# A vision tower on one core: tokenizer differences taken from PSUM, first units as rows come, and unread products in four waits of TensorE

## The chip, the cores and the metric

The kernel runs on one NeuronCore of a Trainium2 chip. The metric is device time in microseconds of one execution, and lower is better. The engines are TensorE (PE, with PEld for its weight loads), VectorE (DVE), ScalarE (ACT), GpSimd (POOL) and SyncE (SP, which only issues transfers here). Each engine works through its own list of instructions in order and waits on semaphores for the others. L12 is line 12 of the kernel.

## The reference, cut to what matters

A batch of 128 images of 128 x 128 goes through a tokenizer (two strided convolutions, each followed by a batch normalization) and two layers. All is float32.

```python
x = _bn(_conv(X, w1, 8), g1, b1, m1, v1)          # 8x8 patches, 64 channels
x = _bn(_conv(x, w2, 2), g2, b2, m2, v2)          # 4x4, stride 2, 256 channels
h = tokens(x)                                     # (128, 64, 256)
h = h + _L0_attn_ref(_layernorm(h), ...)          # sum_d relu(q - k) w_d, softmax, values
h = h + _L0_ffn_ref(_layernorm(h), ...)           # attention by 4 soft experts
h = h + _L1_attn_ref(_layernorm(h), ...)          # linear attention over the batch
h = h + _L1_ffn_ref(_layernorm(h), ...)           # 8 experts, one for each token, capacity 1280
```

In the last step each token goes to the expert with the largest gate; `pos`, a running count of the tokens of each expert, gives its place, and places past the capacity are dropped.

## The kernel before, in words

The stages follow one another: `tokenizer` (0 to 181 us of the span), `relu_attention` (to about 1116), `expert_attention` (to about 1945), `linear_attention` (to about 2275), `route` (to 2324) and `experts`.

**Tokenizer.** Sixteen rows of patches come in one after another (`load`, L82, three buffers). `conv1(r)` (L130) makes two float32 products of 512 columns with the weights `w1bd`, which hold the 64 x 64 matrix twice on the diagonal: an even half and an odd half, each in a PSUM tile `pa`. The even half is scaled and offset by ScalarE into `ev` (L135), shifted by one position on the upper 64 partitions, where a memset has left a zero at the border. The odd half is scaled and offset by VectorE into `h[:, 0:4]` (L132). `differences(r)` then forms even minus odd and odd minus the next even on VectorE (L141, L142). These sums and differences serve a scheme that does the 4-tap second convolution with three products in place of four in each direction. `between` (L151, L154) forms differences of two rows, on GpSimd except for one that VectorE and one that ScalarE takes.

A `Unit(m, ab)` is a quarter of the output channels for two output rows. It has three sets of products, `products(0)`, `(1)` and `(2)` (L177, tile `pc`[...]), each with one ScalarE reading (L189) and one or two VectorE readings (L204, L200), and two `results` (L210), where the scale of the second normalization comes in. Products 0 need the row differences `between(m, 0, ...)`, products 1 the rows themselves and `w02`, products 2 `between(m, 2, ...)`.

The order on each engine is written out by hand (`tc.manual_schedule()`): rows 0 to 4 go through `conv1` and `differences` first, with the row differences of the first units, and only then come the 16 units, each with one more row in front of it as long as there are rows.

**End of attention.** The last block of queries goes through `less_max`, `exponents`, `sums`, `weights` (VectorE, ScalarE, VectorE, GpSimd L535) and then `transpose` on TensorE (L544), `transposed` (ScalarE L552). After it come the products with the values (`po`, L441), their copies (L452), transposes (`pto`, L459) and the additions to `h` (L469). The PSUM pool `psq` (tag `pq`, three buffers) is the one for keys, values and the transposes at a block's beginning.

**Routing.** `route` computes probabilities and places on VectorE. Two small products (`pp`, L1684, L1685) add up the counts across partitions; `past` (L1735) and `bexp` (L1739) give each block of 256 tokens its expert. Then a table of the tokens' numbers by place is made by 64 products `pi` (L1733) of two one-hot matrices: `lh` (L1723) and `hv` (L1726) come from VectorE in groups of eight, two buffers of each, ScalarE multiplies `hv` by the token numbers (L1731), and TensorE sums. The indices `rin` and `rout` (L1742 to L1746) are read from `pi`.

**Experts.** Each block of 256 tokens is gathered by GpSimd (`gather`, L1810), normalized (`moments` L1820, `normal` L1828), transposed (`pt` L1841, copy `xt` L1844), and goes through two layers (`ph` L1853, `po` L1869). Weights come by SP (L1797, L1798), three blocks deep.

Of the kernel before, what the change touches and what calls it, by code (L numbers as in the profile page):

```python
# [26 lines left out]
BLK = 256  # L27
# [4 lines left out]
class Ctx:  # L32
# [3 lines left out]
    def __init__(self, tc, const):  # L36
# [6 lines left out]
        self.zero = const.tile([P, 8], F32, name="zero")  # L43
        nc.vector.memset(self.zero, 0.0)

    def tables(self, const):


        self.rin = const.tile([P, NTILE], I32, name="rin")
        self.rout = const.tile([P, NTILE], I32, name="rout")  # L50
        self.bexp = const.tile([P, NBLK + 1], I32, name="bexp")


def bcast(ap, axis, n):

    v = ap.unsqueeze(axis)
    shape = list(v.shape)
    shape[axis] = n
    return v.to_broadcast(shape)


def tokenizer(c, x, w1, bn1, w2, bn2):
# [6 lines left out]
    with (  # L69
# [2 lines left out]
        tc.tile_pool(name="th", bufs=8) as hp,  # L72
        tc.tile_pool(name="tv", bufs=6) as vp,
        tc.tile_pool(name="tz", bufs=2) as zp,
        tc.tile_pool(name="tp1", bufs=2, space=PSUM) as ps1,
        tc.tile_pool(name="tp2", bufs=3, space=PSUM) as ps2,
    ):
        rows = {}
# [4 lines left out]


        w1bd = wp.tile([P, P], F32, name="w1bd")
        nc.vector.memset(w1bd, 0.0)
        bnv1 = wp.tile([P, 4], F32, name="bnv1")
        bnv2 = wp.tile([P, 4, 4], F32, name="bnv2")
        for k in range(2):
            nc.sync.dma_start(w1bd[k * 64 : (k + 1) * 64, k * 64 : (k + 1) * 64], w1)  # L90
            nc.sync.dma_start(bnv1[k * 64 : (k + 1) * 64, :], bn1)
        load(0, nc.scalar)
        for r in range(1, 3):
            load(r)
# [22 lines left out]
        for ev in evens:  # L117
            nc.gpsimd.memset(ev[0:64, 4], 0.0)
            nc.gpsimd.memset(ev[64:128, 0], 0.0)

        parts = {}

        def conv1(r):

            xt = rows.pop(r)
            parts[r] = h = hp.tile([P, 12, B], F32, tag="h", name="h")
            ev = evens[r % 3]
            for k in range(2):
                pa = ps1.tile([P, 4, B], F32, tag="pa", name="pa")
                nc.tensor.matmul(pa, w1bd, xt[:, 4 * k : 4 * k + 4], start=True, stop=True)  # L130
                if k:
                    nc.vector.tensor_scalar(h[:, 0:4], pa, s1, o1, ALU.mult, ALU.add)  # L132
                else:
                    for o, i in ((ev[0:64, 0:4], slice(0, 64)), (ev[64:128, 1:5], slice(64, P))):
                        nc.scalar.activation(o, pa[i], AF.Identity, bias=o1[i], scale=s1[i])  # L135
            if r + 3 < 16:
                load(r + 3)

        def differences(r):
            h, ev = parts[r], evens[r % 3]  # L140
# [21 lines left out]
        class Unit:  # L162
# [6 lines left out]
            def products(self, i):  # L169
                m, ab = self.m, self.ab  # L170
                pc = ps2.tile([P, 4, 4, N], F32, tag="pc", name="pc")
                for j, j0 in ((1, 0), (0, 4), (2, 8)):
                    for k in range(2):
                        u = w02[:, k, j] if i == 1 else w[:, k + i, j]
                        for par in range(2):
                            r = slice(par * 64, par * 64 + 64)
                            nc.tensor.matmul(  # L177
                                pc[r, j],
                                u[:, ab * 64 : ab * 64 + 64],
                                part(m, i, k)[:, j0 : j0 + 4, r],  # L180
                                start=(k == 0),
                                stop=(k == 1),
                            )
# [5 lines left out]
                nc.scalar.activation(  # L189
                    y,  # L190
                    pc[:, 1].rearrange("p o n -> p n o"),
                    AF.Identity,
                    bias=o2[:, a] if i == 1 else 0.0,
                    scale=s2[:, a] if i == 1 else 1.0,
                )
                o = self.z[:, i].rearrange("p n (o q) -> p n o q", q=2)
                x = pc[:, 0::2].rearrange("p q o n -> p n o q")
                if i == 1:
                    for q in range(2):
                        nc.vector.scalar_tensor_tensor(  # L200
                            o[:, :, :, q], x[:, :, :, q], s2[:, a], y, ALU.mult, ALU.add
                        )
                else:
                    nc.vector.tensor_add(o, x, bcast(y, 3, 2))  # L204

            def results(self, k):

                ab = self.ab
                f = ab // 2 * 128 + (2 * self.m + k) * 16 + ab % 2 * 8
                nc.vector.scalar_tensor_tensor(  # L210
                    h2[:, :, f : f + 8],
                    self.z[:, 2 * k],
                    (s2, n2)[k][:, ab : ab + 1],
                    self.z[:, 1],
                    ALU.mult,
                    ALU.add,
                )

        with tc.manual_schedule():
            for r in range(5):  # L220
                conv1(r)
                if r == 1:
                    nc.gpsimd.tensor_add(w[:, :, 1], w[:, :, 0], w[:, :, 2])
                differences(r)
                if r == 1:
                    nc.scalar.mul(w[:, :, 2], w[:, :, 2], -1.0)
                    nc.gpsimd.tensor_add(w02, w[:, 0:2], w[:, 2:4])
                    between(0, 0, 0)
                elif r == 2:
                    between(0, 0, 1)  # L230
            for k in range(2):
                between(0, 2, k)
# [27 lines left out]
def relu_attention(c, wqkv, wmlp, bmlp):  # L260
# [8 lines left out]
    with (  # L269
# [387 lines left out]
        with tc.manual_schedule():  # L657
# [978 lines left out]
def route(c, k, gfd):  # L1636
# [5 lines left out]
    with (  # L1642
# [56 lines left out]
        nc.vector.tensor_sub(first, end, nblk)  # L1699
        nc.vector.tensor_scalar_mul(first, first, float(BLK))  # L1700


        nc.vector.tensor_add(cs, cs, bcast(pp[:, 0], 1, T))
        nc.vector.scalar_tensor_tensor(oh, cs, float(CAP), oh, ALU.is_le, ALU.mult)
# [14 lines left out]
        for t0 in range(0, T, T // NQ):  # L1719
# [11 lines left out]
                nc.scalar.activation(hv[:, i], hv[:, i], AF.Copy, scale=k.token[:, t])  # L1731
            for i in range(T // NQ):
                nc.tensor.matmul(pi, lh[:, i], hv[:, i], start=(t0 + i == 0), stop=(t0 + i == T - 1))  # L1733
            if t0 == 0:
                nc.vector.tensor_tensor(past, bcast(k.blk, 2, E), bcast(end, 1, NBLK), ALU.is_ge)  # L1735
                nc.vector.tensor_reduce(be[:, 0:NBLK], past, AX.X, ALU.add)
                nc.vector.tensor_scalar_min(be[:, 0:NBLK], be[:, 0:NBLK], float(E - 1))
                nc.vector.tensor_copy(be[:, NBLK : NBLK + 1], end[:, E - 1 : E])
                nc.vector.tensor_copy(c.bexp, be)  # L1739
# [9 lines left out]
def experts(c, hx, gfd, out, w1, w2, b2, routing):  # L1749
# [9 lines left out]
    with ExitStack() as nest:  # L1759
# [138 lines left out]
        with tc.manual_schedule():  # L1898
            for n in range(2):
                blocks[n].load()  # L1900
            for n in range(2):
                blocks[n].gather((False,))
            blocks[0].moments()
            blocks[0].normal()
            blocks[0].transpose()
            for n in range(2):
                blocks[n].gather((True,))
            blocks[1].moments()
            blocks[2].gather()
            blocks[1].normal()  # L1910
# [42 lines left out]
def layout(**i):  # L1953
# [9 lines left out]
    o["w1"] = i["L0_tok_w1"].reshape(64, 64)  # L1963
    o["bn1"] = np.stack([i[f"L0_tok_{k}1"] for k in "gbmv"], axis=1)
# [5 lines left out]
    o["bn2"] = bn2.reshape(4, 8, 2, 8, 2).transpose(1, 3, 0, 2, 4).reshape(64, 4, 4)  # L1970
    q, k, v = (i[f"L0_attn_W{n}"].T for n in "qkv")

    v = v.reshape(D, 32, 8).transpose(0, 2, 1).reshape(D, D)
# [45 lines left out]
```

## Time and profile before

| | us |
|---|---|
| median of three runs | 2759.32 (2752.79 to 2761.09) |
| profiled execution | 2759.04 |
| its span | 2757.1 |
| mean granted clock of TensorE | 0.972 |
| busy: TensorE, VectorE, GpSimd, ScalarE | 2599.0, 2037.6, 1631.1, 1627.6 |

The profiled execution is one run; its time is 1.9 us more than its span, which reaches from the first instruction to the last. A line of the timeline has the start, the length, the engine, the source line, the operation, the output and inputs, the shapes, how many instructions are merged, and in brackets how long the engine was idle before it and what ended that idle time. A line of a table of stretches has the stretch, its length, the busy time of PE, PEld, DVE, ACT and POOL with the number of instructions, the granted clock (1.00 is full), the DMA share and GB/s. A float32 product leaves two records.

### The profile page before, as it was taken

The numbers are of one execution on the slowest core, as the hardware profiler recorded it, in microseconds if no ns is written. First come the engines' busy times: TensorE is split into PE (matmuls) and PEld (weight loads), VectorE is DVE, ScalarE is ACT, GpSimd is POOL, SyncE is SP. The second block draws the span as 40 slices with busy tenths as digits, with TensorE's granted clock in tenths as the row PEclk, the third lists the DMA queues.
The fourth block names the chain that finished last, engine by engine and source line by source line (L and its number), as shares of the span: only waits on it lengthen the run. The fifth ranks groups of instructions, "written<-read, shape, count | busy, mean of one in ns | idle before, by whom it ended". The sixth has DMA issues, their size and how long they took to land. (4 is left out here: it accounts for less than half of the span.)

```text
span 2757.1 us, 76948 instructions
## 1 busy us (share of the span) xinstructions
PE 2599.0 (94%) x33263; PEld 1741.0 (63%) x33263; DVE 2037.6 (74%) x3024; ACT 1627.6 (59%) x3415; POOL 1631.1 (59%) x1390
## 2 busy tenths in 40 slices
PE   7989999999999999799999999999699986999997
PEld 3553434434444443688888888888466565888886
DVE  6759999999998989577877777777367685344443
ACT  3228888888898888366666666566245543233332
POOL 3328888898888888656566565553233312454444
PEclk9999999999999999799999999999899995999999
DMA  3000000000000000000000000000424443555554
GB/s 108 32 12 2 2 1 2 2 2 2 1 2 1 2 2 1 12 11 18 11 11 18 11 15 14 10 19 11 115 62 112 102 120 114 180 197 189 188 196 134
DMA packets 138063, 140.80 MB, mean 51 GB/s; under 512 B 107923, under 2 KB 121509, under 8 KB 130032
## 3 DMA queue, kind: packets, MB, share of 16 engines
q1 hardware_dynamic: 126816, 117.91, 14.3%
q0 software_dynamic: 7648, 14.77, 1.7%
q8 instruction: 263, 4.31, 0.7%
q10 hardware_dynamic: 3248, 3.09, 0.4%
q14 instruction: 88, 0.72, 0.1%
HBM read 103.93 MB, written 32.54 MB: 49 GB/s over the span
## 5 line engine op out<-in xcount | busy, mean ns | idle before, releaser
L495 POOL TENSOR_TENSOR m<-q,k 128x1024 f32<-128x1024 f32 x384 | 719.0, 1903 | 30.5 <-PE sc L297 16.1
L487 DVE TENSOR_TENSOR m<-pc,k 128x2048 f32<-128x2048 f32 (+1 forms) x320 | 646.7, 2058 | 0.5 <-ACT q L431 0.5
L297 PE MATMUL sc<-m,wide 128*32 128x512 f32 x4096 | 529.5, 598 | 12.0 <-DVE m L487 7.2
L496 ACT ACTIVATE m<-m 128x1024 f32<-128x1024 f32 x384 | 402.3, 1049 | 6.0 <-POOL m L495 5.4
L297 PEld LDWEIGHTS sc<-m,wide 128*32 128x32 f32 x4096 | 126.4, 109 | 259.7 <-issue 145.6
L505 ACT ACTIVATE m<-k,q 128x64 f32<-128x64 f32 x1024 | 270.8, 339 | 0.8 <-DVE k L378 0.8
L946 DVE TENSOR_REDUCE mx<-sc 128x16 f32<-128x1024 f32 x128 | 156.1, 1220 | 153.9 <-PE sc L934 123.7
L961 POOL TENSOR_TENSOR e<-e,mx 128x1024 f32<-128x1024 f32 x128 | 243.5, 1902 | 10.1 <-POOL mx L960 0.2
L906 ACT COPY qk<-pqk 128x512 f32<-128x512 f32 x256 | 138.9, 604 | 131.7 <-PE pqk L902 131.7
L960 POOL TENSOR_TENSOR mx<-mx,gate 128x16 f32<-128x16 f32 x128 | 27.6, 216 | 314.5 <-ACT z L991 151.2
L1853 PE MATMUL ph<-xt,w1s 128*128 128x256 f32 x896 | 201.1, 383 | 4.2 <-DVE xt L1844 3.4
L1869 PE MATMUL po<-w2s,hT 128*128 128x256 f32 x896 | 198.0, 379 | 0.0
L973 ACT COPY pT<-pt 128x512 f32<-128x512 f32 x256 | 138.7, 599 | 98.9 <-PE pt L970 98.1
L1853 PEld LDWEIGHTS ph<-xt,w1s 128*128 128x128 f32 x896 | 171.7, 192 | 29.5 <-DVE xt L1844 4.2
L1869 PEld LDWEIGHTS po<-w2s,hT 128*128 128x128 f32 x896 | 168.1, 190 | 21.7
L902 PE MATMUL pqk<-xT,w 64*128 64x128 f32 x2048 | 168.9, 288 | 2.1 <-issue 2.0
L947 DVE TENSOR_TENSOR e<-sc,mx 128x1024 f32<-128x1024 f32 x128 | 156.8, 1225 | 4.4
L1887 POOL DMA_INDIRECT out<-y,rout x56 | 56.7, 1013 | 168.6 <-ACT hT L1857 131.3
L1857 ACT ACTIVATE hT<-ph,w1s 128x256 f32<-128x256 f32 x224 | 93.3, 470 | 104.0 <-PE ph L1853 104.0
L902 PEld LDWEIGHTS pqk<-xT,w 64*128 64x128 f32 x2048 | 142.2, 189 | 19.7 <-issue 10.7
L953 DVE TENSOR_REDUCE mx<-e 128x16 f32<-128x1024 f32 x128 | 153.2, 1197 | 1.7 <-ACT e L950 1.7
L970 PE MATMUL pt<-ident,e 128*128 128x128 f32 x1024 | 142.1, 279 | 6.4 <-POOL e L961 2.8
(302 smaller groups left out, 4976.0 us busy)
## 6 DMA issues: line engine op xcount, KB each, us to landing
w1s<-in_we SPq DMA_DIRECT2D x30, 1028.0 KB, 5.3
w2s<-in_we SPq DMA_DIRECT2D x30, 1024.0 KB, 4.9
hd<-h SPq DMA_DIRECT2D x16, 512.0 KB, 3.2
x<-hd SPq DMA_DIRECT2D x16, 512.0 KB, 3.8
h<-hd SPq DMA_DIRECT2D x4, 2048.0 KB, 12.9
hx<-h SPq DMA_DIRECT2D x4, 2048.0 KB, 11.7
out<-h SPq DMA_DIRECT2D x4, 2048.0 KB, 20.5
xt<-in_x SPq DMA_DIRECT2D x15, 512.0 KB, 3.5
```

Source lines behind the costliest of these rows:

```text
L297: nc.tensor.matmul(dst[j : j + 32], wide[:, hf, s : s + 32], part, start=start, stop=stop)
L487: nc.vector.tensor_tensor(m, bcast(self.pq[:, hf, i : i + n], 3, T), k, ALU.max)
L495: nc.gpsimd.tensor_tensor(m, bcast(self.q[:, hf, s : s + 2], 3, T), k, ALU.subtract)
L496: nc.scalar.activation(m, m, AF.Relu)
L505: nc.scalar.activation(self.parts[i, hf][:, q], self.blk.k[:, hf, i], AF.Relu, bias=self.q[:, hf, i - NB // 2, q : q + 1], scale=-1.0,)
L902: nc.tensor.matmul(pq[par][:, k, eh, :], w[r, f : f + P], self.xT[r, fc], start=True, stop=True)
L946: nc.vector.tensor_reduce(mx, sc, AX.X, ALU.max)
L947: nc.vector.tensor_sub(e, sc, bcast(mx, 2, T))
L953: nc.vector.tensor_reduce(self.sm[x], self.e[x], AX.X, ALU.add)
L961: nc.gpsimd.tensor_mul(e, e, bcast(sm, 2, T))
L1853: nc.tensor.matmul(ph[:, j], self.w1[:, w0 : w0 + P], self.xt[:, fc], start=(fc == 0), stop=(fc == 1))
L1869: nc.tensor.matmul(po, self.hT[:, f, r * P : r * P + P], self.w2[:, f, :], start=(f == 0), stop=(f == 7))
```

## The change

In the tokenizer: the weights, the normalization values and their doubling come ready from the host, so that each is one transfer. The two halves of a row have a PSUM tile of their own (`pa0`, `pa1`). ScalarE writes the even half with the scale only, the border holds minus the offset (written by GpSimd), and the differences are read from the odd half in PSUM, with the reversed sign; the odd half itself is stored negated. The sign is undone with the scale of the second normalization (`n2` for `s2`), and the negation of `w[:, :, 2]` on ScalarE goes. The written order is new: the first unit's products come after row 2, and rows 3 to 6 stand between the sets of products of the first two units.

In four places TensorE gets products that nobody reads (`busy`): six of 128 columns at the start of the tokenizer, five of 512 columns at the end of attention before the last `transpose`, six of 312 columns in `route` after `past`, six of 512 columns before the first block of the experts. In `route` the lines of `past` and `bexp` stand further up in the source.

```diff
+    def busy(self, out, x, n):
+        for _ in range(n):
+            self.nc.tensor.matmul(out, self.ident, x, start=True, stop=True)
...
-        tc.tile_pool(name="tp1", bufs=2, space=PSUM) as ps1,
+        tc.tile_pool(name="tp1", bufs=1, space=PSUM) as ps1,
...
-        nc.vector.memset(w1bd, 0.0)
-        for k in range(2):
-            nc.sync.dma_start(w1bd[k * 64 : (k + 1) * 64, k * 64 : (k + 1) * 64], w1)
-            nc.sync.dma_start(bnv1[k * 64 : (k + 1) * 64, :], bn1)
+        nc.sync.dma_start(w1bd, w1)
+        nc.sync.dma_start(bnv1, bn1)
...
-        for k in range(2):
-            nc.scalar.dma_start(bnv2[k * 64 : (k + 1) * 64], bn2)
+        nc.sync.dma_start(bnv2, bn2)
...
+        ns1, no1 = (wp.tile([P, 1], F32, name=n) for n in ("ns1", "no1"))
+        nc.vector.tensor_scalar_mul(no1, o1, -1.0)
+        nc.vector.tensor_scalar_mul(ns1, s1, -1.0)
...
-                pa = ps1.tile([P, 4, B], F32, tag="pa", name="pa")
+                pa = ps1.tile([P, 4, B], F32, tag=f"pa{k}", name="pa")
                 nc.tensor.matmul(pa, w1bd, xt[:, 4 * k : 4 * k + 4], start=True, stop=True)
                 if k:
-                    nc.vector.tensor_scalar(h[:, 0:4], pa, s1, o1, ALU.mult, ALU.add)
+                    nc.vector.tensor_scalar(h[:, 0:4], pa, ns1, no1, ALU.mult, ALU.add)
+                    odd[r] = pa
                 else:
                     for o, i in ((ev[0:64, 0:4], slice(0, 64)), (ev[64:128, 1:5], slice(64, P))):
-                        nc.scalar.activation(o, pa[i], AF.Identity, bias=o1[i], scale=s1[i])
+                        nc.scalar.activation(o, pa[i], AF.Identity, bias=0.0, scale=s1[i])
...
-            nc.vector.tensor_sub(h[:, 4:8], ev[:, 0:4], h[:, 0:4])
-            nc.vector.tensor_sub(h[:, 8:12], h[:, 0:4], ev[:, 1:5])
+            for j in range(2):
+                nc.vector.scalar_tensor_tensor(
+                    h[:, 4 * j + 4 : 4 * j + 8], pa, s1, ev[:, j : j + 4], ALU.mult, ALU.subtract
+                )
...
-            for r in range(5):
-                conv1(r)
-                if r == 1:
-                    nc.gpsimd.tensor_add(w[:, :, 1], w[:, :, 0], w[:, :, 2])
-                differences(r)
...
+            c.busy(ps1.tile([P, 4, B], F32, tag="pa1", name="idle")[:, 0], c.ident, 6)
+            for ev in evens:
+                for r, j in ((slice(0, 64), 4), (slice(64, P), 0)):
+                    nc.gpsimd.tensor_scalar(ev[r, j], c.ident[r], c.zero[r, 0:1], no1[r], ALU.mult, ALU.add)
+            conv1(0)
+            differences(0)
+            conv1(1)
+            nc.gpsimd.tensor_add(w[:, :, 1], w[:, :, 0], w[:, :, 2])
+            nc.gpsimd.tensor_add(w02, w[:, 0:2], w[:, 2:4])
+            differences(1)
+            conv1(2)
+            between(0, 0, 0)
+            differences(2)
+            between(0, 0, 1)
...
+            units = [Unit(0, ab) for ab in range(2)]
+            units[0].products(0)
+            conv1(3)
+            units[0].products(1)
+            differences(3)
+            between(0, 2, 0)
+            units[0].results(0)
+            units[1].products(0)
+            conv1(4)
+            units[1].products(1)
+            differences(4)
+            between(0, 2, 1)
+            units[1].results(0)
+            conv1(5)
+            units[0].products(2)
+            differences(5)
+            units[0].results(1)
+            between(1, 0, 0)
+            conv1(6)
+            units[1].products(2)
+            differences(6)
+            units[1].results(1)
             for m in range(4):
-                for ab in range(4):
+                for ab in range(0 if m else 2, 4):
...
             old.weights()
+            c.busy(psq.tile([P, 8, T], F32, tag="pq", name="idle"), blocks[-1].k[:, 0, 0:8], 5)
             old.transpose()
...
+        nc.vector.tensor_copy(c.bexp, be)
+        idle = gpp.tile([P, NBLK, E], F32, name="idle")
+        c.busy(idle, past, 6)
...
                 blocks[n].gather((False,))
+            c.busy(psh.tile([P, 2, BLK], F32, tag="ph", name="idle"), blocks[0].w1[:, 0:512], 6)
             blocks[0].moments()
```

More of the change, by code (lines that the diff above doesn't have):

```diff
@@ L114, in tokenizer @@
         s1, o1 = scale_offset(lambda i: bnv1[:, i : i + 1], [P, 1], "1")
+        ns1, no1 = (wp.tile([P, 1], F32, name=n) for n in ("ns1", "no1"))
+        nc.vector.tensor_scalar_mul(no1, o1, -1.0)
+        nc.vector.tensor_scalar_mul(ns1, s1, -1.0)
         evens = [wp.tile([P, 5, B], F32, name=f"ev{k}") for k in range(3)]
[L117 to L121, printed above, removed]
+        parts, odd = {}, {}
         def conv1(r):
@@ L139, in differences @@
         def differences(r):
-            h, ev = parts[r], evens[r % 3]
-            nc.vector.tensor_sub(h[:, 4:8], ev[:, 0:4], h[:, 0:4])
-            nc.vector.tensor_sub(h[:, 8:12], h[:, 0:4], ev[:, 1:5])
+            h, ev, pa = parts[r], evens[r % 3], odd.pop(r)
+            for j in range(2):
+                nc.vector.scalar_tensor_tensor(
+                    h[:, 4 * j + 4 : 4 * j + 8], pa, s1, ev[:, j : j + 4], ALU.mult, ALU.subtract
+                )
         taken = {}
@@ L193, in products @@
                     bias=o2[:, a] if i == 1 else 0.0,
-                    scale=s2[:, a] if i == 1 else 1.0,
+                    scale=n2[:, a] if i == 1 else 1.0,
                 )
@@ L200, in products @@
                         nc.vector.scalar_tensor_tensor(
-                            o[:, :, :, q], x[:, :, :, q], s2[:, a], y, ALU.mult, ALU.add
+                            o[:, :, :, q], x[:, :, :, q], n2[:, a], y, ALU.mult, ALU.add
                         )
@@ L212, in results @@
                     self.z[:, 2 * k],
-                    (s2, n2)[k][:, ab : ab + 1],
+                    (n2, s2)[k][:, ab : ab + 1],
                     self.z[:, 1],
@@ L219, in tokenizer @@
         with tc.manual_schedule():
-            for r in range(5):
-                conv1(r)
-                if r == 1:
-                    nc.gpsimd.tensor_add(w[:, :, 1], w[:, :, 0], w[:, :, 2])
-                differences(r)
[L225 to L232, printed above, removed]
+            c.busy(ps1.tile([P, 4, B], F32, tag="pa1", name="idle")[:, 0], c.ident, 6)
[12 more added lines that the diff above has]
+            between(0, 0, 1)
             s2, o2 = scale_offset(lambda i: bnv2[:, i, :], [P, 4], "2")
@@ L1700, in route @@
         nc.vector.tensor_scalar_mul(first, first, float(BLK))
+        nc.vector.tensor_tensor(past, bcast(k.blk, 2, E), bcast(end, 1, NBLK), ALU.is_ge)
+        nc.vector.tensor_reduce(be[:, 0:NBLK], past, AX.X, ALU.add)
+        nc.vector.tensor_scalar_min(be[:, 0:NBLK], be[:, 0:NBLK], float(E - 1))
+        nc.vector.tensor_copy(be[:, NBLK : NBLK + 1], end[:, E - 1 : E])
+        nc.vector.tensor_copy(c.bexp, be)
+        idle = gpp.tile([P, NBLK, E], F32, name="idle")
+        c.busy(idle, past, 6)
         nc.vector.tensor_add(cs, cs, bcast(pp[:, 0], 1, T))
@@ L1733, in route @@
                 nc.tensor.matmul(pi, lh[:, i], hv[:, i], start=(t0 + i == 0), stop=(t0 + i == T - 1))
[L1734 to L1739, printed above, removed]
         id1 = gp.tile([P, NTILE], F32, name="id1")
@@ L1962, in layout @@
     o["x"] = np.concatenate(x, axis=1)
-    o["w1"] = i["L0_tok_w1"].reshape(64, 64)
-    o["bn1"] = np.stack([i[f"L0_tok_{k}1"] for k in "gbmv"], axis=1)
+    o["w1"] = np.zeros((P, P), np.float32)
+    for k in range(2):
+        o["w1"][k * 64 : k * 64 + 64, k * 64 : k * 64 + 64] = i["L0_tok_w1"].reshape(64, 64)
+    o["bn1"] = np.tile(np.stack([i[f"L0_tok_{k}1"] for k in "gbmv"], axis=1), (2, 1))
     w2 = i["L0_tok_w2"].reshape(4, 4, 64, 8, 2, 8, 2).transpose(0, 1, 2, 4, 6, 3, 5).reshape(4, 4, 64, D)
@@ L1968, in layout @@
     bn2 = np.stack([i[f"L0_tok_{k}2"] for k in "gbmv"], axis=0)
-    o["bn2"] = bn2.reshape(4, 8, 2, 8, 2).transpose(1, 3, 0, 2, 4).reshape(64, 4, 4)
+    o["bn2"] = np.tile(bn2.reshape(4, 8, 2, 8, 2).transpose(1, 3, 0, 2, 4).reshape(64, 4, 4), (2, 1, 1))
     q, k, v = (i[f"L0_attn_W{n}"].T for n in "qkv")
```

## The prediction

> **What bounds the kernel now.** First the page's second part, the span in 40 slices of 68.9 us.
>
> ```profile
> PE   7989999999999999799999999999699986999997
> PEclk9999999999999999799999999999899995999999
> ```
>
> TensorE (PE) is busy nearly everywhere, so a transfer or a VectorE (DVE) instruction saves nothing by itself. But its granted clock dips in slice 17 (from attention to the expert attention), 29 and 34 (routing, first experts), and slice 1 (the tokenizer's start) is short of work. The change puts products without a reader into slice 1, slice 17 and, twice, slice 34, so I read the timeline there, beginning with TensorE alone.
>
> ```profile
> 7.90 3.75 PE L130 MATMUL pa<-xt,w1bd 128*128 128x512 f32 x4 [7.90 <-DMA w1bd<-in_w]
> ...
> 34.85 2.81 PE L177 MATMUL pc<-v,w 128*64 128x256 f32 x24
> ```
>
> The first row's two products (x4: a float32 product leaves two records) start when w1bd lands, and take 3.75 us where 1.98 is usual later (row 6, at 42.77). The first unit's products start only at 34.85; from there TensorE has no gap to 180, and a unit takes 9.84 us: 7.92 of `pc` products, 1.92 of conv1.
>
> ```profile
> 560.06 1.49 PE L441 MATMUL po<-at,v 64*32 64x64 f32 x128
> ...
> 569.60 1.15 PE L544 MATMUL pt<-ident,e 128*64 128x64 f32 x32
> ...
> 1103.05 1.98 PE L544 MATMUL pt<-ident,e 128*64 128x64 f32 x32 [4.64 <-POOL e L535]
> ...
> 1105.71 2.12 PE L441 MATMUL po<-at,v 64*32 64x64 f32 x130 [0.69 <-ACT at L552]
> ```
>
> The first two lines are from the middle of attention, the others from its end. There TensorE waits 4.64 us, and then the same transposes take 1.98 instead of 1.15 us and 130 value records 2.12 where 128 took 1.49. In stretches of 1 us the granted clock is 1.00 until about 1102.1 and 0.50 from there.
>
> ```profile
> 2295.43 27.59 PE L1733 MATMUL pi<-hv,lh 128*128 128x78 f32 x128 [8.05 <-ACT hv L1731]
> ...
> 2302.57 1.22 DVE L1723 TENSOR_TENSOR lh<-lo,at 128x1024 f32<-128x1024 f32 x1 [1.47 <-PE pi L1733]
> 2303.72 0.80 DVE L1726 TENSOR_TENSOR hv<-lo,at 128x624 f32<-128x624 f32 x1
> 2304.61 2.11 ACT L1731 ACTIVATE hv<-hv,token 128x78 f32<-128x78 f32 x8 [1.31 <-DVE hv L1726]
> ```
>
> Routing: the 64 `pi` products run 27.59 us, all at clock 0.50. VectorE's next table waits for them (1.47 us), ScalarE (ACT) needs only 2.11 us for a group of eight. TensorE sets this stage: 3.42 us a group, 0.214 a record.
>
> ```profile
> 2332.75 9.63 PE L1853 MATMUL ph<-xt,w1s 128*128 128x256 f32 x32 [0.78 <-DVE xt L1844]
> ...
> 2348.89 0.43 DVE L1820 BATCH_NORM_STATS2 st<-g 128x6 f32<-128x256 f32 x1 [5.37 <-DMA g<-hx,rin]
> ...
> 2352.30 7.17 PE L1853 MATMUL ph<-xt,w1s 128*128 128x256 f32 x32 [2.58 <-DVE xt L1844]
> ```
>
> First expert block: its products take 9.63 us cold, the next block's 7.17. But that block starts late: its copy `xt` stood on VectorE behind the moments of block 3, which waited for a gather until 2348.89.
>
> [...]the clock is half or full[...]: 0.50 or 1.00; it fell 3.7 us after the work stopped at 1098.4 and about 4.5 after 2176.2, and rose 3.2 us after work began at 187.58, about 5 after 2332.75. [...]`pi` is busy for 27 us and stays at 0.50, so the trace adds that thin products (78 columns against loads of 128) don't warm it. Whether thin work keeps a warm clock, the windows show:
>
> ```profile
> 1930.00:1934.00 4.00, 1.16 (x19) 0.96 (x14) 3.93 (x5) 1.87 (x3) 0.63 (x2) 1.00 0.00 0
> 1942.00:1946.00 4.00, 1.39 (x6) 0.88 (x6) 0.42 (x1) 0.00 (x0) 0.00 (x0) 1.00 0.31 105
> ```
>
> 29% and 35% busy in 4 us, still 1.00. [...]the difference L142 took 3.91 us at 17.93 while GpSimd ran, L200 from PSUM 0.86 for two beside GpSimd at 71.40.
>
> **The change, part by part.** I sum against the profiled execution, 2759.04 us (span 2757.10 and 1.94 around it); the median of the runs is 2759.32, so the sum serves for it too.
>
> *Tokenizer.* Removed: one of two w1bd and bnv1 issues on SP each, two bnv2 issues on ACT's queue (0.52 each; one goes to SP behind row 2, about 0.6 us, ahead of row 3, which waits for a buffer anyway), the memset, a scaling of w on ACT (1.06). Six memsets on GpSimd become tensor_scalars that wait for the offset; w's additions (2.34 and 3.90) follow them and still end by about 16. Differences were 0.68 each and become 512 elements from PSUM: L132 (one PSUM input) is 0.81, L200 0.48 for 256; I take 0.75, bounds 0.68 to 0.95. [...]
> Chain: w1bd issued at 0.8 plus 5.2 (its landing before): 6.0. bnv1 at 1.4 plus 5.0 (3.8 to 6.5): 6.4; scale 7.4, offset and its negative 8.0. Table load 1.28, even half 1.57: 10.3. Two differences: 12. Now row 1: its even half may start at 10.4, but its odd half needs the PSUM tile that the differences of row 0 held: 12.1, done 13, plus 0.35 to the reader, 0.81, 1.5: 15.7. Row 2: 19.2. The vector difference of parts 0 and 2 (1.76): first unit at 21, against 34.85: 13.9 sooner. Given back: conv1 of rows 3 to 5 then comes inside the units, 3 x (1.92 + 0.3) = 6.7. And new waits: rows 5, 6 and 7 wait for the differences of the row before, which stand on VectorE behind an eviction (about 0.5 to ScalarE, 0.4 to 0.56 there, 0.7 to 0.9 on VectorE, then 1.5): about 2 us each less the 0.96 that the even half covers, 4.5 to 6.5 in all, and unit 0's third product waits 1.0 for the last vector difference. Between 16.6 and 21 TensorE idles, 4.4 us, so its clock probably falls[...]. Sum: 13.9 - 6.7 - 6.5 - 1.8 = -1.1, or +2 with short latencies and a clock that stays. I take **0**, between 4 slower and 5 faster. Steady units keep 9.84: in the tightest one differences end at 71.48, the next odd half starts at 73.2, 1.7 of slack. Six idle products at the start (12 records at 0.21 cold, 2.6 us from 1.5) end before w1bd lands; their gain is inside the chain's 1.57 of ScalarE: 0, at most 1.8.
>
> *End of attention.* Five 128x512 products, 0.86 each at full clock (two records at 0.43): 4.3 us from 1098.4 to 1102.7, inside the wait to 1103.05. Nothing is delayed; `psq` is unused then. With the clock up: transposes 0.83, two value runs 2.12 to 1.49 and 2.46 to 1.49, the output's transposes then bound by VectorE's additions at 0.70 instead of 0.86, four times 0.16. Sum: 0.83 + 0.63 + 0.97 + 0.65 = **3.1**, on the chain, since the next stage's weights, moments and GpSimd's factors start behind it (L765 at 1115.64). Bounds 0[...] and 4.
>
> *Routing.* `past` already stood at 2289.14 and keeps its place in VectorE's order; only six 128x312 products are new: 0.52 a record cold, 6.2 us, 2289.7 to 2295.9 at worst, 0.5 beyond the first `pi`. Full columns for 6 us should warm the clock (3.2 to 5 above). Then a record costs 0.11 (the 128x128 transposes at full clock: four in 0.43), a group 1.7, and the ring of two buffers binds: VectorE 1.95, ScalarE 2.11, a last product and latencies 0.4, 4.5 for two groups. Eight groups: 2.2 + 7 x 2.2 = 17.7 instead of 27.6: **9.9 gained**, between -0.6 (not warmed, delay only) and 10.4 (ScalarE's 2.11 alone).
>
> *First experts.* Six 128x512 products start behind `pi`, 5.2 us warm, inside 7.8 (6.9 to 8.6 if cold, then 0.8 late at most). Block 0 gains 0.4 + 2.6, but GpSimd's gathers, one after another, don't move, and block 1 waits for `xt`. The built order of VectorE's instructions moves that copy ahead of block 3's factors: after the second moments, 2350.6, 1.7 sooner. That is all that passes on. The wait before it grows from 2.6 to about 4.2, which may halve the clock again[...]: **1.2**, bounds -1 and 3.
>
> Sum: 0 + 3.1 + 9.9 + 1.2 = 14.2; 2759.0 - 14.2 = **2744.8 us**.
>
> **Rivals.** *A: `pi` stays cold.* For it: it never warmed in 27 us[...]. Against it: stretches at a third of the work kept 1.00. Then routing loses 0.5, the experts' products start cold (0.4 left): 0 + 3.1 - 0.5 + 0.4, **2756**.
> *B: the held PSUM tile binds each unit (slower).* Place: conv1's odd half, every row. The slack is 1.7 us; if differences from PSUM are dearer than taken[...] it is gone. To cost 2 us in each of 14 units: +28 - 14, **2773**. It decides from 1.0 us a unit beyond the slack. Against it: L200's 0.86 beside GpSimd.
> *C: the tokenizer gains what its start promises.* If the waits of rows 5 to 7 hide, 6 more: **2739**.
>
> **How the numbers follow.** The main case 0.68, C 0.08, A 0.16, B 0.08. A measurement of this kernel can tell about 0.3%, 8.3 us, from no change (the three runs lie within 8.3). Main and C are faster but for a tail of 0.04 in which tokenizer and experts both lose; a few hundredths of A fall either way. Faster 0.74, same 0.17, slower 0.09. The range: C and a little below, 2735, up to A, 2757; B and the tails left out.
>
> **What would show it.** Right: `pi` near 17.7 us at clock 1.00; the value runs at 1110 at 1.49; first `pc` products near 21 us; waits of 1 to 2 us on the odd half of rows 5 to 7; the tokenizer's last product within 4 us of 180. Wrong: `pi` still at 0.214 a record (A); unit times above 9.84 with TensorE waiting for L146 of the new kernel (B); or a gain in the routing that the experts' gathers give back.

## The result, and the profile after

The changed kernel takes 2744.55 us (median of six runs, 2743.42 to 2745.41) against 2755.96 for the kernel before (six runs, 2749.43 to 2761.09): a ratio of 0.9954, 95% interval [0.9941, 0.9967]. (Ratios are the record's; the quotient of two medians can differ from them, here 0.9959, below by up to 0.0011.) It is faster by about 0.5%, and 2744.8 had been forecast. The profiled execution took 2744.63 us, its span is 2742.5 against 2757.1, and the mean granted clock 0.981 against 0.972.

The span in 40 slices, as the page of the changed kernel has it:

```profile
PE   7989999999999999799999999999699986999997
PEclk9999999999999999899999999999899998999998
```

PE is the same in every digit: in the slices the change shows in the clock alone, where slice 34 (routing, first experts) goes from 5 to 8 and slice 17 (end of attention) from 7 to 8. In the last one the clock falls at 2728.4 us, behind TensorE's last product (it ends at 2724.2). The timeline of the changed kernel, TensorE alone, shows the tokenizer:

```profile
5.05 1.98 PE L133 MATMUL pa<-xt,w1bd 128*128 128x512 f32 x4 [0.70 <-DMA xt<-in_x]
...
15.87 0.65 PE L183 MATMUL pc<-v,w 128*64 128x256 f32 x4 [0.79 <-ACT v L157]
19.09 4.54 PE L183 MATMUL pc<-v,w 128*64 128x256 f32 x20 [2.57 <-DVE v L160]
...
39.20 1.13 PE L133 MATMUL pa<-xt,w1bd 128*128 128x512 f32 x2 [1.89 <-DVE h L146]
...
45.90 1.12 PE L133 MATMUL pa<-xt,w1bd 128*128 128x512 f32 x2 [1.47 <-DVE h L146]
...
52.34 1.13 PE L133 MATMUL pa<-xt,w1bd 128*128 128x512 f32 x2 [1.52 <-DVE h L146]
```

Row 0 starts at 5.05 instead of 7.90, the first unit at 19.09 (four records of it at 15.87) instead of 34.85. But these records run at half clock: 20 take 4.54 us, where 24 take 2.81 later. The last three lines are the predicted waits on the odd half of rows 5, 6 and 7, 4.9 us together. What is left of 15.8 us is 1.1: the last tokenizer product starts at 178.32 instead of 179.44. The end of attention, TensorE alone:

```profile
1098.31 4.56 PE L49 MATMUL idle<-k,ident 128*128 128x512 f32 x10
1103.32 1.15 PE L574 MATMUL pt<-ident,e 128*64 128x64 f32 x32 [0.45 <-POOL e L565]
1105.16 1.50 PE L471 MATMUL po<-at,v 64*32 64x64 f32 x130 [0.69 <-ACT at L582]
1107.30 1.17 PE L471 MATMUL po<-at,v 64*32 64x64 f32 x96 [0.64 <-ACT oT L482]
1109.51 0.45 PE L471 MATMUL po<-at,v 64*32 64x64 f32 x30 [1.04 <-issue]
```

The idle products fill the wait, the transposes take 1.15 and the first value run 1.50, as in the middle of attention. The second run has a wait of 1.04 us in it that the profile puts down to nothing. Routing, all engines:

```profile
2287.77 5.25 PE L49 MATMUL idle<-past,ident 128*128 128x312 f32 x12 [2.29 <-DVE past L1733]
...
2293.53 4.20 PE L1772 MATMUL pi<-hv,lh 128*128 128x78 f32 x32 [0.50 <-ACT hv L1770]
...
2295.77 1.22 DVE L1762 TENSOR_TENSOR lh<-lo,at 128x1024 f32<-128x1024 f32 x1 [0.83 <-PE pi L1772]
...
2298.22 4.20 PE L1772 MATMUL pi<-hv,lh 128*128 128x78 f32 x32 [0.49 <-ACT hv L1770]
```

Two groups of eight `pi` products (x32) now take 4.20 us and wait 0.49 for ScalarE: 2.345 us a group instead of 3.42. The granted clock is the third column from the end of these stretches of 0.8 us:

```profile
2291.00:2291.80 0.80, 0.80 (x3) 0.52 (x2) 0.77 (x2) 0.00 (x0) 0.00 (x0) 0.67 0.11 10
2291.80:2292.60 0.80, 0.80 (x4) 0.57 (x3) 0.80 (x2) 0.00 (x0) 0.00 (x0) 1.00 1.05 175
```

It rises at about 2291.5, while the last idle products run, and is full to the end of `pi`. The first experts, from the timelines of TensorE, VectorE, SyncE and GpSimd in this order:

```profile
2312.32 5.39 PE L49 MATMUL idle<-w1s,ident 128*128 128x512 f32 x12 [0.52 <-PE pi L1772]
...
2321.11 7.17 PE L1886 MATMUL ph<-xt,w1s 128*128 128x256 f32 x32 [0.79 <-DVE xt L1877]
...
2337.44 7.17 PE L1886 MATMUL ph<-xt,w1s 128*128 128x256 f32 x32 [1.81 <-DVE xt L1877]
```

```profile
2335.84 0.43 DVE L1853 BATCH_NORM_STATS2 st<-g 128x6 f32<-128x256 f32 x1 [3.48 <-DMA g<-hx,rin]
```

```profile
2329.18 0.33 SPq L1830 DMA_DIRECT2D w1s<-in_we  x1
```

```profile
2331.78 1.21 POOL L1843 DMA_INDIRECT g<-hx,rin  x1 [0.20 <-issue]
```

Block 0's products run at full clock (warm), 7.17. Block 1 starts 16.33 us behind block 0, where it was 19.55. The gather of block 3 is read 4.06 us after GpSimd issued it; before, 5.94 (2342.95 to 2348.89).

Where the time came from in this pair of profiles, by how much sooner the same instruction starts: 1.1 us at the first transposes of attention (186.45 against 187.58), but 0.1 at 227 us, since the clock is at half there for 10.2 us instead of 6.8; 0.02 at 1096 us, 2.1 at the next stage's first scores (1139.00 against 1141.13), 1.9 at `pl`, TensorE's first products of the routing (2273.64), 11.2 when VectorE writes `rin` (2311.83 against 2323.05), 14.9 at block 1 (2337.44), and 14.6 at the end.

### The profile page after: what moved, and what is told of

It is laid out like the page before. It is cut to its first block, busy times and chain, and to the rows that moved or that the text cites. A ratio compares the mean times of both kernels' runs of the same rounds, so it can differ in the third digit from the quotient of the medians.

```text
span 2742.5 us, 77026 instructions
## 1 busy us (share of the span) xinstructions
PE 2598.4 (95%) x33309; PEld 1733.3 (63%) x33309; DVE 2027.9 (74%) x3025; ACT 1623.1 (59%) x3414; POOL 1633.7 (60%) x1390
## 3 DMA queue, kind: packets, MB, share of 16 engines
q1 hardware_dynamic: 126928, 117.95, 14.2%
## 5 line engine op out<-in xcount | busy, mean ns | idle before, releaser
L991 POOL TENSOR_TENSOR mx<-mx,gate 128x16 f32<-128x16 f32 x128 | 27.6, 216 | 314.8 <-ACT z L1022 144.3
```

## The experiments

Every kernel was timed together with the kernel before. Over 76 more runs that one took 2749.4 to 2765.3 us, so its median differs between the three sets (2757.78, 2755.65, 2760.61); ratios are to the kernel before of the same set, and steps of 1 to 4 us are read from landmarks in the traces, that is, from where the same instruction starts.

### Which part does it: the tokenizer alone, the idle products alone

Tokenizer alone (x1): the new kernel without its four runs of idle products.

```
-            c.busy(ps1.tile(...)[:, 0], c.ident, 6)
...
-            c.busy(psq.tile(...), blocks[-1].k[:, 0, 0:8], 5)
...
-        c.busy(idle, past, 6)
...
-            c.busy(psh.tile(...), blocks[0].w1[:, 0:512], 6)
```

> The new kernel without its four runs of idle products: the tokenizer's part of the change is left, and the earlier place of past. My theory: the tokenizer reaches its last product about 1 us sooner and the attention gives that back at its start, so the time is the old kernel's, 2755 to 2758 us, with pi at 27.6 us and the value run at the end of attention at 2.1 to 2.5. Rival: the tokenizer's part is worth some us by itself (4 to 6), then 2750 to 2752.

Measured: 2758.87 us, ratio 1.0006 [0.9998, 1.0014], `pi` 27.60. Idle products alone (x2): the four `busy` lines, and the earlier place of `past`, put into the old kernel.

> The old kernel with the four runs of idle products put in at the same places, its tokenizer untouched. Theory: nearly the whole gain is theirs, so 2743 to 2746 us, as the new kernel: end of attention 2.1 to 2.4 sooner, routing 9.3, first experts 3.6. Rival: the new tokenizer carries a part of the 11 us between the medians, then 2747 to 2752.

Measured: 2745.75 us, ratio 0.9963 [0.9951, 0.9975], so 10 us of the gain (7 to 14) without the new tokenizer. From `pp` to block 1's products it takes 52.93 us, the new kernel 52.96 (from the line below to 2337.44), the old one 65.92 (2286.38 to 2352.30):

```profile
2284.48 0.57 PE L1715 MATMUL pp<-cs,before 128*128 128x8 f32 x2 [8.90 <-issue]
```

So the idle products carry the change. Those at the start of the tokenizer were not left out alone; x1, which lacks them, starts attention at 185.55, within the range of the runs with them (185.53 to 186.75). The tokenizer's share isn't nothing in the traces: attention's first transposes start at 185.53 to 186.75 us in eight executions with it (mean 186.03) and at 187.58 and 188.78 in the two without. In the time of 21 runs none of these 2 us shows. The trace of x1 has the clock at half for 6.8 us from about 1146.6 and for 3.4 us from about 1931.7, where the old kernel's profile has it full. That such falls take the gain back on average was not shown.

### Is it the clock: without the routing's idle products, and with narrow ones

Without (x3): `c.busy(idle, past, 6)` is left out. Narrow (x4):

```
-        c.busy(idle, past, 6)
+        c.busy(idle[:, 0:10], past[:, 0:10], 12)
```

> The new kernel without the six idle products of the routing alone; past stays in its new place. Theory: pi runs its 27.6 us at half clock again and rin is 9 us later, so 9 us slower than the new kernel, 2753 to 2754 us; the experts' idle products start cold but still warm their first products. Rival: a clock carried over from elsewhere, or past's new place, is behind the gain: then under 3 us slower.

> The new kernel with the routing's six idle products of 312 columns replaced by twelve of 80 columns, each two records of about 0.215 us: TensorE is busy as long (about 5.2 us) over the same stretch, but with narrow products like those of pi. Theory: a product of some 80 columns spends its time on the load of its weights[...], so the clock stays at 0.50, pi takes 27.6 us, and the time is about 9 us above the new kernel's, 2753 to 2754. Rival: [...]pi stayed cold for another reason: then pi about 18 us and 2744 to 2746.

Measured: x3 2755.13 us, 0.9994 [0.9984, 1.0005]; x4 2753.42 us, 0.9995 [0.9984, 1.0006]. From `pp` to block 1's products, x3 takes 62.25 and x4 62.46 us: 9.3 and 9.5 more than the new kernel, and x3 still 3.7 less than the kernel before, with the idle products of the experts. TensorE in x3:

```profile
2283.58 0.57 PE L1715 MATMUL pp<-cs,before 128*128 128x8 f32 x2 [8.89 <-issue]
...
2292.62 27.60 PE L1770 MATMUL pi<-hv,lh 128*128 128x78 f32 x128 [8.05 <-ACT hv L1768]
...
2345.83 7.17 PE L1884 MATMUL ph<-xt,w1s 128*128 128x256 f32 x32 [1.74 <-DVE xt L1875]
```

TensorE in x4, and a stretch of its clock:

```profile
2285.24 5.41 PE L49 MATMUL idle<-past,ident 128*128 128x80 f32 x24 [2.30 <-DVE past L1733]
2290.99 27.59 PE L1772 MATMUL pi<-hv,lh 128*128 128x78 f32 x128 [0.34 <-ACT hv L1770]
```

```profile
2287.00:2289.00 2.00, 2.00 (x12) 2.00 (x11) 1.86 (x8) 0.00 (x0) 0.00 (x0) 0.50 0.00 0
```

TensorE is as busy ahead of `pi` as in the new kernel, 5.41 us against 5.25, and ends as close to it; the loads of weights fill 5.2 of the 5.41 us. The clock stays at 0.50 and `pi` takes 27.59. So being busy did not raise the clock here: 5.4 us of 80 columns left it at half, 5.3 us of 312 columns raised it. Nor did the products of 80 and 78 columns together, 33 us of them without a longer gap than 0.34.

### How much is needed: three products instead of six (x8)

```
-        c.busy(idle, past, 6)
+        c.busy(idle, past, 3)
```

> The new kernel with three idle products of 312 columns in the routing instead of six: about 2.6 us of work at half clock, then 2.9 us of waiting until pi. Theory: the clock rises only behind a stretch of wide work of more than some 3 us (it rose 3.2 to 5 us after the start of such work), so pi stays at 0.50 and takes 27.6 us: 9 us above the new kernel. Rival: a half of the work is enough, because pi goes on with it: then pi warms in its first few us and takes 18 to 20 us, under 2 us above the new kernel.

Measured: 2752.93 us, ratio 0.9977 [0.9968, 0.9985]. TensorE, and stretches of 0.8 us with the clock in the third column from the end:

```profile
2287.12 3.49 PE L49 MATMUL idle<-past,ident 128*128 128x312 f32 x6 [2.30 <-DVE past L1733]
2292.88 26.36 PE L1772 MATMUL pi<-hv,lh 128*128 128x78 f32 x128 [2.27 <-ACT hv L1770]
```

```profile
2290.00:2290.80 0.80, 0.61 (x2) 0.00 (x0) 0.73 (x4) 0.00 (x0) 0.00 (x0) 0.50 0.00 0
2290.80:2291.60 0.80, 0.00 (x0) 0.00 (x0) 0.80 (x1) 0.00 (x0) 0.00 (x0) 0.73 0.86 113
2291.60:2292.40 0.80, 0.00 (x0) 0.00 (x0) 0.80 (x3) 0.00 (x0) 0.00 (x0) 1.00 0.57 185
...
2294.00:2294.80 0.80, 0.80 (x8) 0.80 (x8) 0.28 (x1) 0.80 (x5) 0.00 (x0) 0.91 0.91 369
2294.80:2295.60 0.80, 0.80 (x6) 0.80 (x5) 0.22 (x1) 0.80 (x5) 0.00 (x0) 0.50 1.05 440
```

`pi` takes 26.36 us, near the 27.6 of the theory, but not for its reason; from `pp` to block 1's products it is 61.64 us, 8.7 more than the new kernel. Three products (3.49 us) did raise the clock, at about 2291.2, when they had already ended. It was up for some 3.4 us, of which TensorE idled 1.7 ahead of `pi`, and fell while `pi` ran. In the new kernel the work ends 0.5 us ahead of `pi`, the clock is up from 2291.5, and the same narrow products keep it for all of the 18 us. So in these two traces the idle products had to reach up to the work that was to profit.

### The end of attention (x6) and the experts (x5), each without its idle products

> The new kernel without the five idle products at the end of the attention. Theory: the last transposes take 1.98 us again, the two value runs 2.12 and 2.46, and the next stage's first scores come 2.1 to 2.4 us later; the time is 2 us above the new kernel's. Rival: the next stage takes the 2 us back, since its clock is half anyway until about 1138 us: then no difference.

> The new kernel itself again, as the measure for the runs beside it and for how much one execution differs from the next. Theory: 2743 to 2747 us; its executions differ by chance in where the clock falls for some microseconds, so the landmarks of this profile lie up to 3 us from those of the first one. Rival: the kernel's landmarks repeat within 0.5 us, and the clock's falls stand at the same places.

Measured: x6 2747.66 us, 0.9967 [0.9956, 0.9979]; the new kernel again, in the same set, 2746.00 us, 0.9962 [0.9949, 0.9974]: not told apart. x6 on TensorE:

```profile
1102.78 1.86 PE L574 MATMUL pt<-ident,e 128*64 128x64 f32 x32 [4.93 <-POOL e L565]
1105.32 1.83 PE L471 MATMUL po<-at,v 64*32 64x64 f32 x130 [0.68 <-ACT at L582]
1107.79 1.30 PE L471 MATMUL po<-at,v 64*32 64x64 f32 x106 [0.64 <-ACT oT L482]
```

Without idle products the clock falls at about 1103, but it is back at 1106.4, within the first value run, where the old kernel's profile had it down until about 1115.7 (and x1, which lacks these products too, until 1109.1): the runs take 1.83 and, with a wait in it, 1.30 and 0.41 instead of 2.12 and 2.46. From the last transposes to the next stage's first scores, x6 takes 36.2 us and x1 36.1; the kernel before took 38.1. With idle products it is 35.2 to 35.8 in eight executions, but 38.0 in x5 and 38.2 in x2, where the clock fell 6.7 us behind the start of these transposes instead of 13 to 14. So the place is worth 0.5 us in most executions, and the 2.1 of the pair of profiles was mostly the 13.7 us at half clock of one execution.

The second profile of the same new kernel lies 0.8 us behind the first at the end of attention and 3.6 behind at `pl` (2277.21): its clock falls for 3.4 us at each of three places (from about 1937, 2200 and 2210 us) where the first has it full. The falls at 2200 and 2210 are in six of the fourteen traces, always both.

> The new kernel without the six idle products ahead of the first expert block. Theory: the clock falls in TensorE's wait behind pi, the first block's products take 9.6 us instead of 7.2, and SyncE's load of a later block's w1s, which waits for these products, is issued on top of block 3's gather again; the gather then lands later and the second block's products start about 14.4 us behind the first's output start again instead of 13.8: in all 2 to 4 us above the new kernel. Rival: the second block waits for VectorE and GpSimd alone, which don't depend on block 0's products: then under 1 us.

Measured: x5 2750.02 us, 0.9960 [0.9946, 0.9973]; the times don't separate it from the new kernel. The trace does: from `pl` to block 1's products 67.86 us instead of 63.80 and (again) 63.57. Its lines, of TensorE, SyncE, GpSimd and VectorE:

```profile
2324.81 9.15 PE L1886 MATMUL ph<-xt,w1s 128*128 128x256 f32 x32 [0.78 <-DVE xt L1877]
...
2344.73 8.86 PE L1886 MATMUL ph<-xt,w1s 128*128 128x256 f32 x32 [3.43 <-DVE xt L1877]
```

```profile
2334.86 0.33 SPq L1830 DMA_DIRECT2D w1s<-in_we  x1
```

```profile
2335.12 1.21 POOL L1843 DMA_INDIRECT g<-hx,rin  x1 [0.20 <-issue]
```

```profile
2340.02 0.43 DVE L1853 BATCH_NORM_STATS2 st<-g 128x6 f32<-128x256 f32 x1 [4.33 <-issue]
...
2341.85 0.43 DVE L1853 BATCH_NORM_STATS2 st<-g 128x6 f32<-128x256 f32 x1 [1.19 <-DMA g<-hx,rin]
```

Block 0 runs in part at half clock (cold, 9.15). SyncE's `w1s` load goes out 0.9 us after these products end, here as in both kernels, and so 0.26 us ahead of the gather of block 3, in the new kernel 2.60 ahead. The gather's two halves are read 4.90 and 6.73 us after its first issue, against 4.06 and 4.62; block 1, whose copy `xt` stands behind them on VectorE, starts 19.92 us behind block 0, and is slow itself (8.86 us, 7.17 in the new kernel). By the landmark the cost, 4.1 to 4.3, is just above the theory's range of 2 to 4 us. Before, the load went out 0.33 us behind the gather's first issue, and the first half was read after 5.94; in the second trace of the new kernel 2.61 ahead, and 3.80. Over all fourteen traces, a load within 0.33 us of the gather goes with a first half read after 4.9 to 5.9 us, one 2.6 to 3.1 ahead with 3.0 to 4.1; between them (1.06, 1.66 and 2.00 ahead) it is 5.30, 3.68 and 4.64. That the load is what delays the gather fits this, with one trace out of line; it wasn't tried by itself.

### Taking the tokenizer's waits away (y2)

```
             conv1(3)
-            units[0].products(1)
             differences(3)
+            units[0].products(1)
```

and the same for rows 4, 5 and 6, so that VectorE has the differences ahead of an eviction.

> The new kernel with the differences of rows 3 to 6 put ahead of the products whose eviction they stood behind on VectorE. Theory: the three waits of TensorE for L146, 1.5 to 1.9 us each, go, and the tokenizer's last product comes 3 to 5 us sooner; the attention's start gives up to 1.5 back by its clock, so the time is 2 to 4 us below the new kernel's. Rival: the evictions behind the differences come later by as much, and TensorE waits for their PSUM tiles instead: no gain.

Measured: 2738.93 us, ratio 0.9940 [0.9927, 0.9952]. TensorE:

```profile
38.10 2.38 PE L183 MATMUL pc<-v,w 128*64 128x256 f32 x20 [0.79 <-DVE v L160]
...
46.91 1.13 PE L133 MATMUL pa<-xt,w1bd 128*128 128x512 f32 x2 [0.71 <-DVE h L146]
```

Of 4.9 us of waits on rows 5 to 7, 0.71 is left, and the wait for the last vector difference (the second of the two `between` that VectorE forms), which the prediction had at 1.0, now shows at 0.79. Attention starts at 181.02 instead of 186.45, and of these 5.4 us nothing is lost: 5.8 at the last transposes of attention (1097.54), 6.3 at `pl`. Some 1.4 of the 5.4 are there ahead of these waits (the second set of the first unit starts at 24.76 instead of 26.21), because the clock at the first unit is at half for 3.4 us instead of 6.8, which is the chance of this profile; y3, with the same order and 6.8 us at half clock, starts attention at 181.66. So the waits, 4 us or more, were the price of the order on VectorE, without them the time comes to rival C's 2739, and attention hands a gain of this size on.

### More places, and a third buffer (y1, y3, y4)

y1 puts idle products of 512 columns ahead of attention (7), ahead of and behind the next attention's weights (2 and 2), and ahead of the last attention (4). y3 is y2 with `bufs=3` for `lh` and `hv`. y4 is y3 with four idle products ahead of the tokenizer's first unit and y1's seven ahead of attention.

> The new kernel with idle products of 512 columns in three more waits of TensorE that are followed by work at half clock: seven ahead of the attention (178.9 to 186.4 us), two ahead of the next attention's weights and two behind them (1113 to 1124 us), four ahead of the last attention (1951 to 1957 us). Theory: what the change's four runs show holds there too. At the attention's start 5.9 us of work at half clock, at the third place about 7, of which half is saved where TensorE sets the pace: 1 to 2.5 and 2.5 to 3.5 us; in the middle 1 to 4. Together 4 to 8, so 2737 to 2741 us. Rival: work at these places waits for other engines, or the idle products come into its way: then within 2 us of the new kernel.

> The new kernel with the differences of rows 3 to 6 ahead of the products, as in y2_differences_sooner, and with three buffers instead of two for the routing's tables lh and hv. Theory: with a warm clock the ring of two binds pi (2.345 us a group of eight); with three ScalarE's 2.11 us a group does, so pi takes 7 x 0.235 = 1.6 us less, and the time is 1.5 to 2 us below y2's 2739: 2737. Rival: VectorE's tables (1.95 us a group and its waits) or the buffers of PSUM bind at once: no difference to y2.

> The kernel y3_sooner_ring3 with idle products in two more waits: four of 512 columns ahead of the tokenizer's first unit (TensorE waits there from 15.1 to 19.1 us, and the clock falls), and seven ahead of the attention (as in y1_idle_more_places). Theory: the first unit's products run at full clock, 2 to 3 us sooner, and the attention's first transposes and keys another 2: up to 5 us below y3, 2732 to 2735, if what stands behind them keeps it. Rival: as in y1_idle_more_places, what is won at the attention's start is gone by its end (0.2 of 2.0 us was left at 1103 us), and only the tokenizer's 2 to 3 stay: 2734 to 2736; or neither: 2737.

Measured: y1 2747.30 us, 0.9967 [0.9954, 0.9979]; y3 2739.74, 0.9929 [0.9915, 0.9942]; y4 2738.00, 0.9927 [0.9913, 0.9940]. y2, y3 and y4 beat both kernels and can't be told from each other.

y1's rival holds. The time is within 2 us of the new kernel's. At the start of attention its products are 2.0 us sooner, and this was there still at 660 us, 1.6 at 890 and 0.15 at 1103; how it goes is told below, with y4. In the next attention the first scores come 3.6 us sooner (1135.43), and the second ones 0.7: the clock, which the new kernel's profile has full there, is at half for 6.8 us from about 1144. At `pl`, behind the last place, it is 0.4. In y3 the ring does what was expected and the next stage takes most of it back. `pi` and block 0 on TensorE:

```profile
2288.00 16.21 PE L1772 MATMUL pi<-hv,lh 128*128 128x78 f32 x128 [0.52 <-ACT hv L1770]
...
2313.58 8.69 PE L1886 MATMUL ph<-xt,w1s 128*128 128x256 f32 x32 [0.78 <-DVE xt L1877]
```

16.21 us instead of 18.27, so 2.03 a group; but the clock falls in the wait behind, and block 0 takes 8.69 instead of 7.17: from `pp` to block 1's products 52.17 us, y2 53.05. In y4, TensorE keeps its clock at the first unit, and loses the time in the middle of attention:

```profile
14.63 3.60 PE L49 MATMUL idle<-h,ident 128*128 128x512 f32 x8
18.16 3.03 PE L183 MATMUL pc<-v,w 128*64 128x256 f32 x24
...
672.88 2.73 PE L328 MATMUL sc<-m,wide 128*32 128x512 f32 x18 [0.73 <-issue]
...
900.48 0.27 PE L472 MATMUL po<-at,v 64*32 64x64 f32 x2 [1.28 <-issue]
```

24 records take 3.03 us, and at 190 us TensorE is 3.8 us ahead of y3. 0.8 of it goes at about 450 us, 1.7 at 672 and 1.5 at 900, each within one step. In the last two, TensorE stands for 0.73 and 1.28 us in a wait that the profile puts down to nothing ("issue"), which y3 has at neither place. The three steps are 16 apart: they end at the 17th, 33rd and 49th of attention's 64 groups of transposes (`pt`). y1 lost its 0.4 and 1.5 us at the last two of them, the 1.5 with a wait of the same kind:

```profile
906.02 2.33 PE L327 MATMUL sc<-m,wide 128*32 128x512 f32 x17 [0.94 <-issue]
```

y1 and y4 are the two programs with idle products ahead of attention. The kernel before, the new one and its second profile, y2 and y3 lose less than 0.5 us to each other at these steps. So, as far as the profile shows, it was not another engine that took y1's gain there, as its rival had it. What this wait is stays open.

## Why the prediction was right, point by point

**Tokenizer: 0 forecast, 1.1 in the pair, about 2 over ten traces, nothing measurable in the time.** First unit at 19.1 instead of 21, since row 0 and w1bd were there by 5.0. Waits 4.9, inside the 4.5 to 6.5 (the prediction's own terms for them, less the 0.96, add up to 6.4 to 7.5). The further wait of 1.0 for the vector difference stood behind them unseen (y2). The cold stretch was the mis-sized term: 1.8 forecast, an estimate of the author's, about 3 measured (20 records in 4.54 us and four conv1 records in 2.72; the clock at half for 6.8 us from 18.2). Beside GpSimd the differences are no dearer: two of them from PSUM took 1.40 us at 67.16, with GpSimd at its additions from 65.76 to 72.63, and 1.40 at 50.89, with GpSimd idle; rival B, which needed them dearer, is out.

**End of attention: 3.1 forecast, 2.1 in the pair, 0.5 by x6 and x1.** The step that failed is taking 2.46 us of the second value run as what every execution pays. It was the course of one execution: at half clock for 13.7 us there, where x1 was for 6.8 and x6 for 3.4.

**Routing: 9.9 forecast, 9.3 in the pair and by x3.** The mechanism was right, the ring of two too: it binds at 2.345 us a group, not 2.2, and y3 takes that away. Rival A is what x3 and x4 look like (`pi` 27.60 and 27.59 us); the idle products avoided it (18.27). The weight it got in the forecast was the author's estimate. The two stretches that the prediction showed for thin work don't show it: 0.7 of the 1.16 us and all of the 1.39 are products of 256 columns. That 78 columns kept the clock is shown by the new kernel's `pi`, for its 18.27 us; in x8 it fell while they ran.

**Experts: 1.2 forecast, 3.6 in the pair, 3.7 by x3, about 4 by x5.** "GpSimd's gathers don't move" was right for their issue and wrong for their landing, which came 1.9 us sooner. The wait ahead of block 1 fell to 1.81 where 4.2 was forecast; what a fall of the clock in it would cost was the author's estimate, and block 1 ran at 7.17 us, as before.

The sum, 14.2 forecast and 14.6 measured, is so close by luck, because misses cancel: 1.2 less than forecast by `pl`, 0.6 less in the routing, 2.4 more in the experts. And the old kernel's profile, 2759.04, on which the sum stands, was among its slower executions, so the medians differ by 11.4 only.

## What to carry to other kernels

Look for work at half clock behind a wait of TensorE, and fill the wait with wide products that end where the work begins (of 312 columns here: six, ending 0.50 us ahead of `pi`, brought it from 27.60 to 18.27 us, three, ending 2.27 ahead, to 26.36); whether the stage keeps what it wins has to be measured. A gain of one or two us at a landmark is worth nothing until it is still there at the end of the next stage: compare several executions, since the clock was at half for 13.7 us in one and for 6.8 and 3.4 in others at the same place (the end of attention, before, x1 and x6), and two traces of the new kernel lie 3.6 us apart at `pl`. Put short work that frees a PSUM tile ahead of a longer eviction in VectorE's order: that reordering alone was worth some 6 us here (0.9940 against 0.9962).

## What the runs showed of the hardware

- Float32 products of 80 and 78 columns, each with its own load of weights, kept TensorE busy for 5.4 and 27.6 us without raising the clock (x4); once it was up by 312-column products, the 78-column ones kept it for 18 us (new kernel).
- The clock rose 4.1 us after 3.5 us of wide products had begun, in the idle time behind them, and fell 3.4 us later, with 78-column products running for the last 1.8 of these (x8).
- The stretches at half clock between the first microseconds and the last product lasted 3.41, 6.83, 10.24, 13.65, 17.07, 20.48 and 64.85 us in the traces of the kernel before and the new one, each a whole number of 3.41 us: 6.8 and 13.7 at the start and the end of attention before, 10.2 at its start in the new kernel. The end of attention had 3.4 in x6, and x5 had 30.7 from 1110 us.
- Two traces of one program (new kernel) differ by 3.6 us at a landmark near 2275 us, with three falls of the clock between that only one of them has.
- TensorE lost 0.7 to 1.3 us at a time in waits for which the profile shows no cause, in y1 and y4 at the same steps of attention.
